# Layer 0's patch spectra in half-array matmuls: two patches in the halves of TensorE's rows, the inverse in the halves of its columns

## The chip, the cores and the metric

One core of a Trainium2 chip (trn2). The metric is the device time of one execution in microseconds (us), the median of several runs. A profile of one execution stands beside it. Lines are those of the kernel before; L512 is line 512. The engines: PE is TensorE's matmuls, PEld its weight loads, DVE is VectorE, ACT ScalarE, POOL GpSimd, SP SyncE.

## The reference, cut to what matters

`x` is 4 images of 48 channels and 256 x 256 pixels, fp32. Four layers follow, each added to its input after a group norm: layer 0 (below), layer 1 (a filter in 8 x 8 patches, a depthwise 3 x 3 convolution, a gated product), layer 2 (box means over learned offsets, from an integral image), layer 3 (a gated convolution and a filter in patches). Layer 0 is

```python
hidden = conv1x1(group_norm(x), w_hidden) + b_hidden          # 48 -> 288 channels
qkv = depthwise3x3(hidden, w_dw) + b_dw
q, k, v = split(qkv, 3, axis=1)                               # 96 channels each
q_patch, k_patch = (t.reshape(B, 96, 32, 32, 8, 8) for t in (q, k))
out = irfft2(rfft2(q_patch) * rfft2(k_patch), s=(8, 8))
out = out.reshape(B, 96, 256, 256)
normed = (out - mean(out, axis=1)) / sqrt(var(out, axis=1) + 1e-5) * gamma + beta
x = x + conv1x1(v * normed, w_out) + b_out
```

The reshape cuts each channel's memory into runs of 64 numbers, so a "patch" is 64 neighbouring pixels of one image row, read as 8 x 8. The product of two spectra is a complex one; the inverse of it is the circular convolution of the two patches.

## The kernel before, in words

The kernel is one program of fully unrolled Python loops under a tile framework, which adds the semaphores, gives tiles their buffers and orders each engine's instructions by a priority that follows the program order. Two streams of work are written into one order. Stream "a" runs layers 0 and 1 of image 0, then of images 1, 2, 3, and at the end layer 3 of all four; stream "b" runs the first statistics, layer 1's weights and layer 2 of each image as soon as layer 1 is done with it. `run` (the loop over `advance`) always takes up the stream whose clock is behind; each generator's `yield n` adds n to its clock. So the instructions of b that stand between two pieces of a are fixed by these numbers and not by the time on the chip, and each engine works its own list in order.

PSUM has 8 banks: a pool of 5 for stream a, 2 for stream b and one for layer 2's weights. `bank()` takes one of the stream's pool; a bank is free again when all that reads it is done.

Layer 0 (`layer0`) handles an image in 128 units of 512 pixels (4 blocks of 128). Its loop runs units n in a software pipeline: in step n it issues

- `convolve` of unit n: the 1x1 and 3x3 convolutions as one matmul over (tap, channel) rows, with pixels as the stationary operand and the 288 output channels moving. `convolve2` has 12 calls on 128 rows (L427) and 4 "tails" on 58 rows (L435), of which two in turn stand in rows 0 to 57 and in rows 64 to 121. Output: 4 banks of 128 pixels x 288 channels, copied by ACT to `qkv` (L508).
- `inverse` of unit n - 2 (L528, L529), then per channel statistics over 96 channels on DVE (`bn_stats`, L531) and a copy of the bank to `o` on ACT (L532); `scales` for a finished pair of units.
- a `yield`, at which stream b may put its instructions in between.
- `spectra` of unit n - 1 (L512 to L520), `turn` of unit n - 5 (4 transposes, L567), `project` of unit n - 6 for every second pair of units (L579), and `gate` of unit n - 4, and a second `yield`.

In `qkv` a partition is a pixel: partitions 0 to 63 are one patch, 64 to 127 the next. A patch of real numbers has 34 real and 30 imaginary parts that matter, 64 numbers. Before the change the two patches of a block share each matmul by a block-diagonal matrix of 128 x 128: `f1` gives in its 128 rows of output both patches' 68 real and 60 imaginary parts. `f2` gives for the products' other half the partners. `spectra` does three matmuls of 128 rows into 128 columns with 384 moving numbers (4 blocks x 96 channels): f1 on q, f1 on k and f2 on k. ACT copies q's spectrum to SBUF (`qs`, L516), DVE makes the two products t1 and t2 (L519, L520) and `inverse` adds a1 on t1 and a2 on t2 in one bank. An fp32 matmul is two instructions on PE in the profile (1024 where the program calls 512).

Of the kernel before, what the change touches and what calls it, by code (L numbers as in the profile page):

```python
# [8 lines left out]
F32 = mybir.dt.float32  # L9
# [49 lines left out]
def constants():  # L59
    own, pairs = _frequencies()  # L60
    every = own + pairs
    cos = {f: _waves(f)[0].ravel() for f in every}
    sin = {f: _waves(f)[1].ravel() for f in every}

    f1, f2, a1, a2 = (np.zeros((128, 128)) for _ in range(4))
    for k in range(2):
        px = slice(64 * k, 64 * k + 64)
        for i, f in enumerate(every):  # L70
            r, w = 34 * k + i, (1 if f in own else 2) / 64
            f1[px, r] = cos[f]
            a1[r, px] = w * cos[f]
            if f in pairs:
                f2[px, r] = -sin[f]
                a2[r, px] = -w * sin[f]
        for i, f in enumerate(pairs):
            r, w = 68 + 30 * k + i, 2 / 64
            f1[px, r] = -sin[f]
            f2[px, r] = cos[f]  # L80
            a1[r, px] = -w * cos[f]
            a2[r, px] = -w * sin[f]

    rf, pick = np.zeros((128, 128)), np.zeros((40, 128))
    at = [(f, True) for f in every] + [(f, False) for f in pairs]
    for j, (f, even) in enumerate(at):
        wave = (cos if even else sin)[f].reshape(8, 8) * (1 if f in own else np.sqrt(2)) / 8
        for k in range(2):  # L90
            block = np.zeros((8, 16))
            block[:, 8 * k : 8 * k + 8] = wave
            rf[:, 64 * k + j] = block.ravel()
            u, v = f
            if f in own or v in (1, 2, 3):
                pick[5 * u + v, 64 * k + j] = 1
            else:
                pick[5 * u + v, 64 * k + j] = pick[5 * (8 - u) + v, 64 * k + j] = 0.5

    sel = np.zeros((CP, 4, 112))
    tapsel = np.zeros((112, 4, 106))
    for g in range(4):
        for p in range(112 if g < 3 else 96):
            if g < 3:
                tap, ch = 3 * (p // 48) + g, p % 48
            else:
                tap, ch = 6 + p // 32, 16 + p % 32
            tapsel[p, g, 96 + tap] = 1  # L110
            sel[ch, g, p] = 1


    sel2 = np.zeros((CP, 4, 122))
    tapsel2 = np.zeros((128, 4, 74))
    sel2_full = np.zeros((CP, 3, 128))
    for g in range(3):
        for p in range(128):
            tap, ch = 3 * (p // 48) + g, p % 48
            sel2_full[ch, g, p] = 1  # L120
            for q in (0, 64):
                tapsel2[p, g, q + tap] = 1
    for p in range(48):
        sel2[32 + p % 16, 3, [10 + p, 74 + p]] = 1
        for q in (0, 64):
            tapsel2[10 + p, 3, q + 6 + p // 16] = 1
    sel2 = np.concatenate([sel2_full.reshape(CP, -1), sel2[:, 3]], 1)


    inside = np.ones((10, 256, PW))  # L130
    for t in range(9):
        if t // 3 == 0:
            inside[t, 0] = 0
        if t // 3 == 2:
            inside[t, -1] = 0
        if t % 3 == 0:
            inside[t, :, 0] = 0
        if t % 3 == 2:
            inside[t, :, 255] = 0

    group = np.zeros((CP, CP))
    for i in range(CP):
        for h in range(2):
            j = 48 * h + i % 48 // 3 * 3
            group[i, j : j + 3] = 1 / 6


    edge = np.zeros((10, 18), int)
    edge[1:9, 1:17] = np.arange(128).reshape(8, 16)
    edge[0, 1:17], edge[9, 1:17] = 128 + np.arange(16), 144 + np.arange(16)  # L150
    edge[1:9, 0], edge[1:9, 17] = 160 + np.arange(8), 168 + np.arange(8)
    edge[0, 0], edge[0, 17], edge[9, 0], edge[9, 17] = 176, 177, 178, 179
    shift = np.zeros((9, 128 + NH, 128))
    for r in range(8):
        for c in range(16):
            for t in range(9):
                shift[t, edge[r + t // 3, c + t % 3], 16 * r + c] = 1


    at128 = np.arange(128)[:, None]  # L160
    down = np.zeros((128, 2, 2, 129))
    along = np.zeros((128, 2, 256))
    for a in range(2):
        for h in range(2):
            down[:, h, a] = 128 * a + at128 <= 128 * h + np.arange(129)[None]
        along[:, a] = 128 * a + at128 <= np.arange(256)[None]


    px = at128 + 128 * np.arange(512)[None]
    centre = np.stack([(px % 256 + 0.5) / 256 * 2 - 1, (px // 256 + 0.5) / 256 * 2 - 1], 1)  # L170
    got = {
        "c_ident": np.eye(128),
        "c_dft": np.stack([f1, f2, a1, a2, rf, rf.T], 1),
        "c_pick": pick,
        "c_sel": sel,
        "c_tapsel": tapsel,
        "c_sel2": sel2,
        "c_tapsel2": tapsel2,
        "c_inside": inside.reshape(10, 256 * PW),
        "c_group": group,  # L180
        "c_shift": shift.reshape(9, -1),
        "c_down": down,
        "c_along": along,
        "c_centre": centre,
    }
    return {k: np.ascontiguousarray(v, dtype=np.float32) for k, v in got.items()}


class Net:
    def __init__(self, ctx, tc, a, out):  # L190
        self.tc, self.nc, self.a, self.out = tc, tc.nc, a, out
        self.nimage = a["x"].shape[0] // C

        self.banks = {
            f: ctx.enter_context(tc.tile_pool(name="ps" + f, bufs=n, space=PSUM)) for f, n in (("a", 5), ("b", 2))
        }
        self.stream = "a"
        self.const = ctx.enter_context(tc.tile_pool(name="const", bufs=1))
        self.dram = ctx.enter_context(tc.tile_pool(name="dram", bufs=1, space=DRAM))
        self.stat = ctx.enter_context(tc.tile_pool(name="stat", bufs=2))  # L200
        self.n = 0
        nc, a = self.nc, self.a
        self.ident = self.load("c_ident", [128, 128])
        dft = self.load("c_dft", [128, 6, 128])
        self.f1, self.f2, self.a1, self.a2, self.rf, self.ri = (dft[:, i, :] for i in range(6))
        self.sel = self.load("c_sel", [CP, 4, 112])
        self.tapsel = self.load("c_tapsel", [112, 4, 106])
        self.group = self.load("c_group", [CP, CP])
        self.eps = self.const.tile([128, 1], F32, name="eps")
        nc.vector.memset(self.eps[:], 1e-5)  # L210
        self.zero = self.const.tile([CP, PW + 4], F32, name="zero")
        nc.vector.memset(self.zero[:], 0.0)
# [253 lines left out]
    def layer0(self, x, mr, y):  # L466
        nc, a = self.nc, self.a
        st = self.stat.tile([CP, 129, 6], F32, name=self.nm("st"), tag="st" + self.stream, bufs=1)
        with ExitStack() as ctx:
            w = ctx.enter_context(self.pool("w0", 1))  # L470
# [37 lines left out]
                        nc.scalar.copy(t.qkv[:, 2 * q + b, :], banks[2 * b + q][:, 0:288])  # L508

            def spectra(t):  # L510
                q1, k1, k2 = self.bank(), self.bank(), self.bank()
                nc.tensor.matmul(v3(q1), self.f1, t.qkv[:, :, 0:96], start=True, stop=True)  # L512
                nc.tensor.matmul(v3(k1), self.f1, t.qkv[:, :, 96:192], start=True, stop=True)
                nc.tensor.matmul(v3(k2), self.f2, t.qkv[:, :, 96:192], start=True, stop=True)
                qs = sb.tile([128, 384], F32, name="qs", tag="qs")
                nc.scalar.copy(qs[:], q1[:, 0:384])  # L516
                t.t1 = sb.tile([128, 384], F32, name="t1", tag="t1")
                t.t2 = sb.tile([128, 384], F32, name="t2", tag="t2")
                nc.vector.tensor_mul(t.t1[:], qs[:], k1[:, 0:384])  # L519
                nc.vector.tensor_mul(t.t2[:], qs[:], k2[:, 0:384])  # L520

            def inverse(t):

                if t.j == 0:
                    t.strip.o = sb.tile([128, 8, 96], F32, name="o", tag="o")
                    t.strip.bs = sb.tile([128, 8, 6], F32, name="bs", tag="bs")
                po = self.bank()
                nc.tensor.matmul(po[:, 0:384], self.a1, t.t1[:], start=True, stop=False)  # L528
                nc.tensor.matmul(po[:, 0:384], self.a2, t.t2[:], start=False, stop=True)  # L529
                for b in range(4):  # L530
                    nc.vector.bn_stats(t.strip.bs[:, 4 * t.j + b, :], po[:, 96 * b : 96 * b + 96])  # L531
                nc.scalar.copy(  # L532
                    t.strip.o[:, 4 * t.j : 4 * t.j + 4, :].rearrange("p a b -> p (a b)"), po[:, 0:384]
                )
# [837 lines left out]
```

## Time and profile before

| what | before |
|---|---|
| median of 3 runs | 20871.12 us (20867.39 to 20881.85) |
| profiled execution | 20882.08 us, span from the first to the last instruction 20880.3 us |
| granted TensorE clock, mean | 0.922 |
| layer 0, first to last copy of qkv, images 0 to 3 | 130 to 1939, 3604 to 5592, 7798 to 9795, 12004 to 14000 us |
| layer 3 (first to last gelu, L1167) | 16207 to 20854 us |
| layer 2's gathers beside it (L1037), images 0 to 3 | 4050 to 7421, 8251 to 11630, 12456 to 15816, 16701 to 19831 us |

How to read the profile's views: a group of instructions is one line of the kernel on one engine with one kind of tile; "busy" is the time in which at least one of the group ran, "mean ns" the mean duration of one, and what follows the second bar is the time the engine stood idle just before them, with what ended it. Matmuls are pipelined, so durations of neighbours overlap and the distance from start to start says what one costs. In a view in order of time each row is a start, a length, the engine, the line, and how many instructions in turn were merged.

### The profile page before, as it was taken

To read this page: it belongs to the slowest core of one execution; us is meant where nothing else is said; L and a number is where in the kernel's file an instruction comes from. 1 tells how busy PE (TensorE), PEld (TensorE's weight loads), DVE (VectorE), ACT (ScalarE), POOL (GpSimd) and SP (SyncE) were. 2 spreads that over 40 slices of the span, in tenths; PEclk is the share of its full clock that TensorE was granted. 3 is DMA by queue.
4 is the path that set the end of the run, shared out by engine and by line. 5 is a ranking of instruction groups with operands and counts; after the bars stand their busy time and mean duration, and the time that the engine had idled before them with its cause. 6 is when DMAs were issued, how large, how long until landed. Compare 5 with 4: busy or idle time off the path is not lost.

```text
span 20880.3 us, 231985 instructions
## 1 busy us (share of the span) xinstructions
PE 18892.3 (90%) x79032; PEld 12001.4 (57%) x79032; DVE 10763.0 (52%) x21931; ACT 5909.3 (28%) x12275; POOL 8637.2 (41%) x8887
## 2 busy tenths in 40 slices
PE   7998798999878989998788899997888999999999
PEld 4565435666533346665433466654334787878888
DVE  4544322477765534677645447776554255555521
ACT  2333312344321123443311234433112211111111
POOL 1000000277754511777555216775552066666600
PEclk9899799999968999999689899996899999999999
DMA  4623886555588975555889755558897566666633
GB/s 114 135 55 82 233 217 194 137 132 134 132 235 230 241 207 139 130 134 127 233 230 240 219 133 130 133 127 229 236 239 225 137 150 151 158 152 160 151 76 74
DMA packets 2444896, 3440.27 MB, mean 165 GB/s; under 512 B 580102, under 2 KB 1997038, under 8 KB 2333179
## 3 DMA queue, kind: packets, MB, share of 16 engines
q1 hardware_dynamic: 1908216, 2084.50, 38.2%
q0 software_dynamic: 452560, 1110.45, 21.1%
q10 hardware_dynamic: 82944, 230.48, 4.4%
q8 instruction: 635, 10.40, 0.2%
q14 instruction: 541, 4.43, 0.1%
HBM read 2486.99 MB, written 802.77 MB: 158 GB/s over the span
## 4 chain that ended last, share of the span: by engine, by line
PE 65%; DMA 15%; DVE 7%; POOL 7%; issue 4%; SPq 1%; ACT 1%; DVEq 0%; ACTq 0%; POOLq 0%
PE ps L427 19%; POOL V L1037 7%; PE ps L947 6%; PE ps L728 5%; PE ps L435 4%; PE ps L741 4%; DMA ct<-cD 4%; PE ps L742 3%; PE ps L697 3%; PE ps L828 3%; DMA hD<-hs 2%; PE ps L1188 2%; DVE V L1050 2%; PE ps L815 1%; PE ps L966 1%
## 5 line engine op out<-in xcount | busy, mean ns | idle before, releaser
L1037 POOL DMA_INDIRECT V<-t,idx x8192 | 8227.0, 1004 | 4897.9 <-issue 2346.8
L427 PE MATMUL ps<-W,A 128*128 128x288 f32 (+1 forms) x24576 | 5547.3, 374 | 85.9 <-DMA A<-x 23.4
L427 PEld LDWEIGHTS ps<-W,A 128*128 128x128 f32 x24576 | 4281.6, 191 | 1226.6 <-issue 523.4
L227 POOL DMA_DIRECT2D X<-x x192 | 144.5, 757 | 4302.6 <-DMA x<-xt 3040.1
L1050 DVE TENSOR_TENSOR V<-V 128x1536 f32<-128x1536 f32 (+3 forms) x2048 | 1839.3, 900 | 19.2
L1048 DVE TENSOR_TENSOR V<-V,w 128x3072 f32<-128x3072 f32 x512 | 1713.3, 3346 | 35.9 <-DMA V<-t,idx 27.0
L728 PE MATMUL ps<-hg,ct 128*128 128x512 f32 x2304 | 1264.4, 676 | 417.5 <-DMA ct<-cD 339.5
L947 PE MATMUL ps<-A,W 112*96 112x512 f32 x3072 | 1544.9, 642 | 26.2 <-DVE xt L1069 21.5
L697 PE MATMUL ps<-win,xp 48*128 48x288 f32 x4096 | 1054.8, 594 | 547.9 <-DVE xp L684 232.4
L508 ACT COPY qkv<-ps 128x288 f32<-128x288 f32 x2048 | 769.9, 400 | 2641.1 <-PE ps L427 1258.4
L435 PE MATMUL ps<-W,B 58*128 58x288 f32 (+1 forms) x8192 | 1271.5, 391 | 26.1 <-DMA B<-x 13.8
L742 PE MATMUL ps<-yh,ht 65*128 65x512 f32 x2304 | 1163.1, 649 | 145.7 <-DMA yh<-ys 111.6
L531 DVE BATCH_NORM_STATS2 bs<-ps 128x6 f32<-128x96 f32 x2048 | 397.4, 251 | 1634.3 <-PE ps L529 1632.3
L741 PE MATMUL ps<-ys,tt 128*128 128x512 f32 x2304 | 1174.1, 632 | 27.6 <-DVE ys L732 25.7
L697 PEld LDWEIGHTS ps<-win,xp 48*128 48x128 f32 x4096 | 647.3, 259 | 924.3 <-ACT hs L704 291.9
L1168 DVE TENSOR_TENSOR gp<-gl,ps 128x192 f32<-128x192 f32 x1024 | 353.8, 351 | 1588.1 <-ACT gl L1167 1579.9
L728 PEld LDWEIGHTS ps<-hg,ct 128*128 128x128 f32 x2304 | 468.0, 211 | 1051.6 <-issue 949.1
L1167 ACT ACTIVATE gl<-ps 128x192 f32<-128x192 f32 x1024 | 332.7, 330 | 2529.4 <-PE ps L427 2245.4
L435 PEld LDWEIGHTS ps<-W,B 58*128 58x128 f32 x8192 | 762.4, 186 | 454.1 <-issue 346.4
L746 DVE TENSOR_TENSOR gt<-gl,ps 128x512 f32<-128x512 f32 x576 | 395.1, 687 | 1142.2 <-PE ps L742 1136.6
L947 PEld LDWEIGHTS ps<-A,W 112*96 112x96 f32 x3072 | 513.9, 176 | 731.4 <-issue 690.3
L742 PEld LDWEIGHTS ps<-yh,ht 65*128 65x128 f32 x2304 | 451.3, 199 | 794.3 <-issue 699.4
(186 smaller groups left out, 24654.4 us busy)
## 6 DMA issues: line engine op xcount, KB each, us to landing
hD<-hs SPq DMA_DIRECT2D x64, 4608.0 KB
hg<-hD SPq DMA_DIRECT2D x288, 1024.0 KB
gD<-gt SPq DMA_DIRECT2D x144, 1024.0 KB
gs<-gD SPq DMA_DIRECT2D x64, 2304.0 KB
V<-t,idx POOLq DMA_INDIRECT x8192
A<-x SPq DMA_DIRECT2D x512, 193.5 KB
xt<-x SPq DMA_DIRECT2D x256, 387.0 KB
A<-x ACTq DMA_DIRECT2D x512, 193.5 KB
```

The lines of the kernel that those rows point to most:

```text
L427: nc.tensor.matmul(to(q, b), A[:, r + q, 128 * b + g : 128 * b + g + 128], W[:, g, :], start=b == 0 and g == 0, stop=b == 1 and g == 2,)
L435: nc.tensor.matmul(to(q, b), B[p, r // 2, 128 * b : 128 * b + 128], W[p, 3, :], start=b == 1, stop=b == 0)
L508: nc.scalar.copy(t.qkv[:, 2 * q + b, :], banks[2 * b + q][:, 0:288])
L697: nc.tensor.matmul(ps[:, :288], xp[64 * h : 64 * h + 48, b, :], win[64 * h : 64 * h + 48], start=True, stop=True,)
L728: nc.tensor.matmul(ps[:].rearrange("p (s n) -> p s n", n=32), ct[:, c, :], hg[:, :, c, :], start=True, stop=True)
L741: nc.tensor.matmul(order(ps[:]), to[:, q, :], pick(yo, 128, q), start=True, stop=False)
L742: nc.tensor.matmul(order(ps[:]), ho[:, q, :], pick(yho, NZ, q), start=False, stop=True)
L828: nc.tensor.matmul(pp[:CP, :], pr[:, q, :], got[q][:], start=q == 0, stop=q == 2)
L947: m = nc.tensor.matmul(ps[:96, :].rearrange("p (r c) -> p r c", c=256), W[: kk[g], g, :], of[: kk[g]], start=g == 0, stop=g == 3,)
L1037: nc.gpsimd.indirect_dma_start(out=V[:, k, 4 * cr : 4 * cr + 4, :].rearrange("p e c -> p (e c)"), out_offset=None, in_=table, in_offset=ba ...
L1048: self.pinned(nc.vector.tensor_mul(Vm, Vm, wm.unsqueeze(2).to_broadcast([128, 64, 48])))
L1050: nc.vector.tensor_add(V[:, :, 0:n, :], V[:, :, 0:n, :], V[:, :, n : 2 * n, :])
```

## The change

Only layer 0's spectra, its inverse and the matrices for them change. There are no block-diagonal matrices any more, but matrices of 64 pixels for one patch. The first, `fq`, gives [f1 | f1]: the 64 numbers of the spectrum, twice; `fk` gives [f1 | f2]. The two halves of the partitions, that is the two patches of a block, are handled by separate matmuls on 64 rows each (rows 0 to 63 and 64 to 127), with an output of 128 partitions in a bank of their own. So q and k take two banks each. For each patch ACT copies q's bank to SBUF and DVE multiplies it with k's bank: one product of 128 x 384 holds both t1 and t2 of that patch. The inverse multiplies it with [a1; a2] (128 rows to 64 columns), patch 0 to PSUM partitions 0 to 63, patch 1 to partitions 64 to 127 of one bank, each in a single call instead of two that add up.

Per unit: spectra's calls 3 on 128 rows before, 4 on 64 rows after; inverse's calls 2 into 128 columns before, 2 into 64 columns after; banks in spectra 3 before, 4 after; copies of q on ACT 1 before, 2 after (each 128 x 384); products on DVE 2 before and after. Buffers for q's copy and the products: two each of 128 x 384 under one tag per patch.

```diff
-    f1, f2, a1, a2 = (np.zeros((128, 128)) for _ in range(4))
-    for k in range(2):
-        px = slice(64 * k, 64 * k + 64)
...
+    f1, f2, a1, a2 = np.zeros((64, 64)), np.zeros((64, 64)), np.zeros((64, 64)), np.zeros((64, 64))
...
+    first, second = np.tile(np.hstack([f1, f1]), (2, 1)), np.tile(np.hstack([f1, f2]), (2, 1))
+    back = np.vstack([a1, a2])
...
-        "c_dft": np.stack([f1, f2, a1, a2, rf, rf.T], 1),
+        "c_dft": np.hstack([first, second, rf, rf.T, back]),
...
-        dft = self.load("c_dft", [128, 6, 128])
-        self.f1, self.f2, self.a1, self.a2, self.rf, self.ri = (dft[:, i, :] for i in range(6))
+        dft = self.load("c_dft", [128, 576])
+        self.fq, self.fk, self.rf, self.ri = (dft[:, 128 * i : 128 * i + 128] for i in range(4))
+        self.back = dft[:, 512:576]
...
-                q1, k1, k2 = self.bank(), self.bank(), self.bank()
-                nc.tensor.matmul(v3(q1), self.f1, t.qkv[:, :, 0:96], start=True, stop=True)
-                nc.tensor.matmul(v3(k1), self.f1, t.qkv[:, :, 96:192], start=True, stop=True)
-                nc.tensor.matmul(v3(k2), self.f2, t.qkv[:, :, 96:192], start=True, stop=True)
-                qs = sb.tile([128, 384], F32, name="qs", tag="qs")
-                nc.scalar.copy(qs[:], q1[:, 0:384])
-                t.t1 = sb.tile([128, 384], F32, name="t1", tag="t1")
-                t.t2 = sb.tile([128, 384], F32, name="t2", tag="t2")
-                nc.vector.tensor_mul(t.t1[:], qs[:], k1[:, 0:384])
-                nc.vector.tensor_mul(t.t2[:], qs[:], k2[:, 0:384])
+                q, k = [self.bank() for _ in range(2)], [self.bank() for _ in range(2)]
+                half = lambda p: slice(64 * p, 64 * p + 64)
+                for to, f, c in ((q, self.fq, 0), (k, self.fk, 96)):
+                    for p in range(2):
+                        nc.tensor.matmul(
+                            v3(to[p]), f[half(p), :], t.qkv[half(p), :, c : c + 96], start=True, stop=True
+                        )
+                t.product = []
+                for p in range(2):
+                    qs = sb.tile([128, 384], F32, name="qs", tag=f"qs{p}")
+                    nc.scalar.copy(qs[:], q[p][:, 0:384])
+                    t.product.append(sb.tile([128, 384], F32, name="tp", tag=f"tp{p}"))
+                    nc.vector.tensor_mul(t.product[p][:], qs[:], k[p][:, 0:384])
...
-                nc.tensor.matmul(po[:, 0:384], self.a1, t.t1[:], start=True, stop=False)
-                nc.tensor.matmul(po[:, 0:384], self.a2, t.t2[:], start=False, stop=True)
+                for p in range(2):
+                    nc.tensor.matmul(
+                        po[64 * p : 64 * p + 64, 0:384], self.back, t.product[p][:], start=True, stop=True
+                    )
```

More of the change, by code (lines that the diff above doesn't have):

```diff
@@ L63, in constants @@
     sin = {f: _waves(f)[1].ravel() for f in every}
-    f1, f2, a1, a2 = (np.zeros((128, 128)) for _ in range(4))
-    for k in range(2):
-        px = slice(64 * k, 64 * k + 64)
[L70 to L82, printed above, removed]
+    f1, f2, a1, a2 = np.zeros((64, 64)), np.zeros((64, 64)), np.zeros((64, 64)), np.zeros((64, 64))
+    for i, f in enumerate(every):
+        w = (1 if f in own else 2) / 64
+        f1[:, i] = cos[f]
+        a1[i] = w * cos[f]
+        if f in pairs:
+            f2[:, i] = -sin[f]
+            a2[i] = -w * sin[f]
+    for i, f in enumerate(pairs):
+        f1[:, 34 + i] = -sin[f]
+        f2[:, 34 + i] = cos[f]
+        a1[34 + i] = -2 / 64 * cos[f]
+        a2[34 + i] = -2 / 64 * sin[f]
+    first, second = np.tile(np.hstack([f1, f1]), (2, 1)), np.tile(np.hstack([f1, f2]), (2, 1))
+    back = np.vstack([a1, a2])
     rf, pick = np.zeros((128, 128)), np.zeros((40, 128))
```

## The prediction, made before the changed kernel was run

> **What bounds the kernel now.** I read the page's busy row first, then the busy time by stage, then the groups of instructions, then the order of time inside one step of layer 0.
>
> ```profile
> PE 18892.3 (90%) x79032; PEld 12001.4 (57%) x79032; DVE 10763.0 (52%) x21931; ACT 5909.3 (28%) x12275; POOL 8637.2 (41%) x8887
> ```
>
> TensorE is the busiest engine, but 90% is a mean over stages. Layer 0 runs in four stretches (first to last copy of qkv, one per image); the second view has the engines' busy time in the first two of them (columns: length, then PE, PEld, DVE, ACT, POOL, granted clock, DMA share, GB/s).
>
> ```profile
> core 0: us, PE busy (x) PEld busy (x) DVE busy (x) ACT busy (x) POOL busy (x), PEclk, DMA share, GB/s
> 130.00:1950.00 1820.00, 1792.55 (x6527) 1093.79 (x6526) 798.91 (x2489) 657.97 (x1607) 72.81 (x138) 0.94 0.36 86
> 3604.00:5613.00 2009.00, 1980.74 (x8135) 1267.33 (x8134) 1280.67 (x2951) 812.46 (x1770) 1131.55 (x1129) 1.00 0.52 132
> ```
>
> PE is busy for 98.5% of both; DVE for 64% and POOL for 56% of the second, where layer 2 of another image runs beside. The third and fourth stretches read like the second. The four make 7865 us, and in them a microsecond of PE is a microsecond of the end, unless a wait takes its place.
>
> The groups of the changed lines, and two that resemble what comes (count | busy, mean ns of one | idle before):
>
> ```profile
> L427 PE MATMUL ps<-W,A 128*128 128x288 f32 (+1 forms) x24576 | 5547.3, 374 | 85.9 <-DMA A<-x 23.4 <-DVE xt L581 19.2 <-DVE z L1203 9.1
> L435 PE MATMUL ps<-W,B 58*128 58x288 f32 (+1 forms) x8192 | 1271.5, 391 | 26.1 <-DMA B<-x 13.8 <-DVE t L519 11.4 <-ACT qkv L508 0.5
> L512 PE MATMUL ps<-qkv,c_dft_sb 128*128 128x384 f32 x1024 | 424.7, 497 | 0.0
> L529 PE MATMUL ps<-t,c_dft_sb 128*128 128x384 f32 x1024 | 416.0, 488 | 0.0
> L516 ACT COPY qs<-ps 128x384 f32<-128x384 f32 x512 | 244.8, 478 | 544.6 <-PE ps L512 451.3 <-issue 32.4 <-DMA A<-x 18.8
> ```
>
> 512 units (128 per image) give 1024 matmuls a line: each fp32 matmul is two passes on PE. L435 already does what the change wants for the spectra: its two calls stand in rows 0 to 57 and 64 to 121. Its matmuls last 391 ns each but cover only 1271.5/8192 = 155 ns apiece; L427's cover 5547.3/24576 = 226. They overlap in pairs.
>
> One step in order of time, PE alone (start us, us, what):
>
> ```profile
> 1003.28 0.81 PE L528 MATMUL ps<-t,c_dft_sb 128*128 128x384 f32 x2
> 1003.92 0.81 PE L529 MATMUL ps<-t,c_dft_sb 128*128 128x384 f32 x2
> 1004.57 0.81 PE L512 MATMUL ps<-qkv,c_dft_sb 128*128 128x384 f32 x2
> 1005.21 0.81 PE L513 MATMUL ps<-qkv,c_dft_sb 128*128 128x384 f32 x2
> 1005.86 0.81 PE L514 MATMUL ps<-qkv,c_dft_sb 128*128 128x384 f32 x2
> 1006.50 0.60 PE L567 MATMUL ps<-c_ident_sb,un 128*96 128x128 f32 x4
> ...
> 1008.66 3.08 PE L427 MATMUL ps<-W,A 128*128 128x288 f32 x12
> 1011.66 1.24 PE L435 MATMUL ps<-W,B 58*128 58x288 f32 x8
> 1012.83 3.18 PE L427 MATMUL ps<-W,A 128*128 128x288 f32 x12
> 1015.85 0.81 PE L528 MATMUL ps<-t,c_dft_sb 128*128 128x384 f32 x2
> ```
>
> From L528 to L567 ten passes take 6.50 - 3.28 = 3.22 us: 0.322 us a pass of 384 columns, start to start, with no gap and all weight loads hidden. A pass of 288 columns should then be 0.322 x 288/384 = 0.2415 us.
>
> **Removed and added passes.** Before: 6 passes in spectra, 4 in inverse, 10 x 0.322 = 3.22 us a unit. After: spectra has 4 calls on 64 rows (8 passes), inverse 2 calls into 64 columns (4 passes). If two halves run at once, spectra is 4 slots, inverse 2: 6 x 0.322 = 1.93 us. Four slots go: 4 x 0.322 x 512 = 659 us.
>
> For the row halves the trace decides: eight passes of L435 take 1012.83 - 1011.66 = 1.17 us; in turn they would take 1.93. For the column halves no row exists: no matmul here writes PSUM from partition 64 with 64 columns or fewer. Bounds: full overlap 0.64 us, as L435; none 1.29 us, as now; over 512 units the two ends differ by 2 x 0.322 x 512 = 330 us. I take full overlap, since L435 is the nearest row, with the same two calls in turn and the same fp32. The doubt is that each partition's data must now be read for two tiles at once, which L435 doesn't do.
>
> **Switches between shapes.** From 1008.66 to 1015.85 there are 24 full passes and 4 slots of pairs: 28 x 0.2415 = 6.76 us, but 7.19 passed. The 0.43 us are the two changes of shape, full to halves and back, 0.21 us each. The Trainium skill (TensorEngine Tiling (Array Packing), Key Properties) says that a change of tiling mode, unlike a change of tile, drains the engine. It speaks against this change and names no price; the row gives it. Left out, the sum would be 659 us; by the row it is halved, as follows. Today spectra and inverse have the convolution's shape and need no switch. After, the order is full, columns, rows, full: 3 switches a unit. In 345 of 512 units L512 follows L529 directly; in 167 a matmul of the other stream stands between, and there it is a fourth. 3 x 512 + 167 = 1703 switches x 0.21 = 358 us. Columns to rows isn't in the trace; I give it the same price (bounds 0.1 and 0.3, so about 50 us to either side).
>
> 659 - 358 = 301 us less PE.
>
> A second rule against it: the skill's TensorE: Matmul & The Clock Gate (Part 3, The mechanism) says weight loads overlap running matmuls only when the row group differs; both column tiles use all rows. By its rule of columns/1.2 ns, four loads of 64 columns are 0.21 us a unit if exposed, an estimate of 109 us. The trace disagrees: L528 to L514 load 128 columns ten times in 3.22 us without a gap, on the same rows. I charge nothing, and keep 109 us for the range.
>
> **ACT and DVE.** One copy of q more per unit: 478 ns x 512 = 245 us on ACT, which is busy 36 to 40% in these stretches: hidden in its idle time; uncovered it would cost all 245. The DVE products stay two of 128x384 (549 ns each, L519 and L520). The constants are loaded once, 576 columns for 768: nothing.
>
> **The banks: a possible new wait.** Stream a has 5 PSUM banks. In spectra the inverse's bank and three others were held, and the transposes (L567) had a free fifth. Now spectra holds four, so L567 must wait until the inverse's bank or the first q bank is free. Behind L567 on PE wait project and the next convolution. The timeline of such a unit:
>
> ```profile
> 4825.18 0.81 PE L529 MATMUL ps<-t,c_dft_sb 128*128 128x384 f32 x2
> ...
> 4826.02 0.76 DVE L531 BATCH_NORM_STATS2 bs<-ps 128x6 f32<-128x96 f32 x4 [7.70 <-PE ps L529]
> ...
> 4826.66 0.48 ACT L516 COPY qs<-ps 128x384 f32<-128x384 f32 x1 [1.54 <-PE ps L512]
> ...
> 4827.04 0.49 ACT L532 COPY o<-ps 128x384 f32<-128x384 f32 x1
> ```
>
> The last inverse pass starts at 4825.50; its bank is free 2.03 us later, at 4827.53. In the new order L567 is due 0.32 + 0.21 + 1.29 + 0.21 = 2.03 us after it: just in time. The first q bank is ready earlier: q's pair ends about 1.33 us after that pass, plus a 0.48 us copy. But DVE and ACT may be held by others. Over all 512 units the release comes on average 2.46 us after; had every L567 to wait for that bank, the mean wait would be 0.52 us, against some 65 us in all (0.13 each) that PE waits for that copy now: +0.39 x 512 = 200 us. At the other end nothing, as the q bank serves. I take 0.1 us a unit, 50 us, nearer to nothing as q's copy usually comes in time. Products held late by DVE (L435 already waits 40 us for them) come about as late as now.
>
> **Sum.** 301 - 50 = 251 us. The profiled execution is 20882.08 us, its span 20880.3; the median is 20871.1, 11 below. 20882 - 251 - 11 = 20620 us, -1.2%.
>
> **Rivals.**
> 1. Column halves run in turn. PE then loses 301 - 330 = 29 us, and with 50 us of waits the kernel is 79 us slower: 20950. Place: the two calls of inverse; it decides once they need over 0.64 + 251/512 = 1.13 us of the possible 1.29. For it: no row of the trace, two streams from each partition. Against: L435's calls of the same form overlap fully. If only the middle passes overlap (3 slots), half is lost: 251 - 165 = 86, 20785.
> 2. The bank wait takes the place: 301 - 200 = 101 us faster, 20770. For it: five banks, all held; 10% of the releases come over 3.85 us after. Against: the q bank.
> 3. DVE or POOL sets the pace where layer 2 runs beside, and only the first image gains: 251 x 1820/7865 = 58 us, 20813. Against: 64% and 56% busy.
> 4. The halves don't do what they say and rows run in turn: 4 more slots, 659 us lost. L435 excludes it.
>
> **Chances.** Main case 0.56, its own range 20530 (no bank wait, switches into 64 columns some 0.05 us cheaper) to 20700 (switches at 0.25 us or so); rival 1 in full 0.22, by half 0.07; rival 2 0.12; rival 3 0.03. The range 20530 to 20945 leaves out about half of rival 1 and a little below: under 2 in 10. About 0.2% can be told from no change, 42 us either way. Faster: the main case and what of the others stays under 20829, 0.70. Within: remains of rivals 1 to 3, 0.08. Slower: rival 1, 0.22.
>
> **What would show it.** The inverse's new line should cover about 160 ns a pass (0.64 us for its four), its two calls starting within some ns; 320 ns means rival 1. The four spectra calls should take 1.29 us from first to last plus the two edges. From the last convolution pass to L567, 2.6 us for 3.22 where no other stream's work lies between. PE's waits before L567 for L532 or the q copy: under 100 us, over 200 is rival 2. The layer-0 stretches should each be some 60 us shorter, layers 1 and 3 unchanged. I am wrong most simply if a pair of columns, or a change from columns to rows, costs more than L435's.

## The result, and the profile after

The changed kernel takes 20835.58 us (median of 20 runs) against 20877.06 us for the kernel before in 20 runs: a ratio of 0.9982, interval 0.9975 to 0.9989. (One run of each took over twice as long, 53574 and 42591 us, and is left out of the ratio.) That is a gain of 41 us where 251 were forecast. It lies inside the range; it is small, but the interval leaves no change out. The profiled execution took 20836.07 us (span 20834.3, mean granted clock 0.917). Lines are now those of the kernel after: the inverse is L534, its statistics L538 and the copy to `o` L539; spectra is L517, the copies of q L523, the products L525, the transposes L574, the projection L586, the convolution L428 and its tails L436.

The page's busy row: TensorE is busy for 300 us less than before.

```profile
PE 18592.2 (89%) x80056; PEld 11483.9 (55%) x80056; DVE 10767.5 (52%) x21931; ACT 6091.5 (29%) x12787; POOL 8608.8 (41%) x8887
```

The same two windows as before the change (length, PE, PEld, DVE, ACT, POOL, granted clock, DMA share, GB/s). In the first, PE has room; in the second it is busy for 1888 of 2009 us where it was for 1981, and its clock has gone from 1.00 to 0.97. The second window ends 73 us behind the changed kernel's own stretch, which is 3531 to 5540 us; that one has 1910 us of PE and a clock of 0.98 (its line stands with the first experiment).

```profile
130.00:1950.00 1820.00, 1742.90 (x6936) 981.51 (x6934) 837.42 (x2565) 723.85 (x1781) 73.18 (x138) 0.92 0.37 90
3604.00:5613.00 2009.00, 1887.85 (x8092) 1111.56 (x8092) 1308.12 (x2983) 844.09 (x1847) 1159.98 (x1153) 0.97 0.52 131
```

The changed groups of matmuls: a third more passes than before in spectra (4096 for 3072), as many as before in the inverse.

```profile
L517 PE MATMUL ps<-qkv,c_dft_sb 64*128 64x384 f32 x4096 | 848.0, 517 | 5.0 <-ACT qkv L509 5.0
L534 PE MATMUL ps<-tp,c_dft_sb 128*64 128x384 f32 x2048 | 447.3, 514 | 15.3 <-DVE tp L525 15.3
```

One step of image 0 in order of time, PE alone. The four passes of the inverse take 0.79 us to the next start, the eight of spectra 1.50. From the inverse to the transposes it is 2.29 us.

```profile
1028.38 0.87 PE L534 MATMUL ps<-tp,c_dft_sb 128*64 128x384 f32 x4
1029.17 1.56 PE L517 MATMUL ps<-qkv,c_dft_sb 64*128 64x384 f32 x8
1030.67 0.64 PE L574 MATMUL ps<-c_ident_sb,un 128*96 128x128 f32 x4
```

So the matmuls do what was hoped; the time goes elsewhere. Worked out from the start times and clock rows of the two traces, for the layer-0 stretch of each image (first to last copy of qkv): its length; the time in it at half clock; and the sum of PE's standstills, which counts each start-to-start distance over 0.75 us, less 0.35 for a pass. A pass of 512 columns takes 0.86 us at half clock and so counts as well: 76 and 82 us of image 0's two sums are of this kind, and 15 us or less of each of the others.

| image | length before | after | half clock before | after | standstills before | after |
|---|---|---|---|---|---|---|
| 0 | 1808.8 | 1746.0 | 228.7 | 273.1 | 109.7 | 140.1 |
| 1 | 1988.1 | 2008.8 | 6.8 | 88.7 | 26.9 | 113.0 |
| 2 | 1997.1 | 2006.1 | 17.1 | 81.9 | 33.9 | 112.6 |
| 3 | 1996.7 | 2003.3 | 17.1 | 75.1 | 33.8 | 108.4 |

Image 0, which has no layer 2 beside it, gains 63 us. The other three are longer by 21, 9 and 7. One of their standstills, in order of time (in brackets how long the engine stood, and for whom):

```profile
4310.98 3.35 DVE L1055 TENSOR_TENSOR V<-V,w 128x3072 f32<-128x3072 f32 x1
...
4311.69 1.56 PE L517 MATMUL ps<-qkv,c_dft_sb 64*128 64x384 f32 x8
...
4314.24 0.75 DVE L538 BATCH_NORM_STATS2 bs<-ps 128x6 f32<-128x96 f32 x4
...
4315.10 0.48 ACT L539 COPY o<-ps 128x384 f32<-128x384 f32 x1 [3.69 <-DVE bs L538]
4315.48 0.87 ACT L523 COPY qs<-ps 128x384 f32<-128x384 f32 x2
...
4315.63 0.64 PE L574 MATMUL ps<-c_ident_sb,un 128*96 128x128 f32 x4 [2.38 <-ACT o L539]
```

DVE is in layer 2's product for 3.35 us (L1055) and reaches the inverse's statistics only then. ACT stands 3.69 us in front of the copy to `o`, because that copy reads the same bank and is made to follow the statistics. Both copies of q stand behind it in ACT's list, although their banks have been full for more than a microsecond. So no bank is free until `o` has been copied, and PE stands 2.38 us in front of the transposes. At 4316.7 us the granted clock falls to half, for 3.4 us.

What ACT and PE wait for in the stretch of image 1 (total us, times, longest), first ACT, then PE, both of the kernel after:

```profile
ACT o L539 <- DVE bs L538: 99.5, 56, 7.0
```

```profile
PE ps L428 <- ACT qs L523: 18.3, 12, 5.4
PE ps L586 <- ACT qs L523: 15.6, 11, 2.2
PE ps L574 <- ACT o L539: 14.7, 10, 3.2
PE ps L428 <- DVE tp L525: 14.2, 5, 5.9
```

And ACT's wait in the same stretch of the kernel before:

```profile
ACT o L532 <- DVE bs L531: 94.8, 52, 4.1
```

ACT's wait for DVE is old: 94.8 us in 52 times. But the fifth bank was free then, and PE stood only 4.3 us for ACT's copies of q and `o`. In the kernel after ACT's wait is on PE's path, and through the banks it reaches the projection and the next convolution as well. The last of PE's rows is a second kind: a bank of k, which is free only when DVE has made the product. Over the whole kernel PE's waits for ACT's copies of q and `o` went from 15.7 to 164.6 us, those for DVE's products from 26.8 to 72.6.

### The profile page after: what moved, and what is told of

Same layout as the page of the kernel before. It is cut to its first block, busy times and chain, and to the rows that moved or that the text cites. A ratio compares the mean times of both kernels' runs of the same rounds, so it can differ in the third digit from the quotient of the medians.

```text
span 20834.3 us, 235001 instructions
## 1 busy us (share of the span) xinstructions
PE 18592.2 (89%) x80056; PEld 11483.9 (55%) x80056; DVE 10767.5 (52%) x21931; ACT 6091.5 (29%) x12787; POOL 8608.8 (41%) x8887
## 4 chain that ended last, share of the span: by engine, by line
PE 62%; DMA 16%; DVE 9%; POOL 7%; issue 4%; SPq 1%; ACT 1%; ACTq 0%; DVEq 0%; POOLq 0%
PE ps L428 19%; POOL V L1044 7%; PE ps L954 5%; PE ps L735 4%; PE ps L436 4%; PE ps L748 4%; DMA ct<-cD 3%; PE ps L749 3%; PE ps L704 3%; PE ps L835 3%; PE ps L1195 2%; DVE V L1057 2%; DVE V L1055 2%; DMA hD<-hs 2%; PE ps L517 2%
## 5 line engine op out<-in xcount | busy, mean ns | idle before, releaser
L428 PE MATMUL ps<-W,A 128*128 128x288 f32 (+1 forms) x24576 | 5612.7, 378 | 184.3 <-ACT qs L523 52.8
L428 PEld LDWEIGHTS ps<-W,A 128*128 128x128 f32 x24576 | 4329.6, 193 | 1351.8 <-issue 554.8
L1055 DVE TENSOR_TENSOR V<-V,w 128x3072 f32<-128x3072 f32 x512 | 1713.9, 3347 | 39.8 <-DMA V<-t,idx 31.7
L436 PE MATMUL ps<-W,B 58*128 58x288 f32 (+1 forms) x8192 | 1239.7, 392 | 28.5 <-DVE tp L525 14.3
L538 DVE BATCH_NORM_STATS2 bs<-ps 128x6 f32<-128x96 f32 x2048 | 398.3, 253 | 1615.1 <-PE ps L534 1614.7
L436 PEld LDWEIGHTS ps<-W,B 58*128 58x128 f32 x8192 | 751.8, 187 | 440.1 <-issue 329.6
L711 ACT COPY hs<-ps 128x288 f32<-128x288 f32 x1024 | 619.3, 657 | 1006.1 <-PE ps L704 824.3
```

Source lines behind the costliest of these rows:

```text
L428: nc.tensor.matmul(to(q, b), A[:, r + q, 128 * b + g : 128 * b + g + 128], W[:, g, :], start=b == 0 and g == 0, stop=b == 1 and g == 2,)
L436: nc.tensor.matmul(to(q, b), B[p, r // 2, 128 * b : 128 * b + 128], W[p, 3, :], start=b == 1, stop=b == 0)
L1055: self.pinned(nc.vector.tensor_mul(Vm, Vm, wm.unsqueeze(2).to_broadcast([128, 64, 48])))
```

## The experiments

The theory ahead of the first runs: the matmuls save what they should, and the lost time is PE waiting for a bank that ACT frees late. Rivals: DVE, with layer 2 beside, sets the pace whatever the banks do; the saving itself is small where another stream interleaves; or half-array matmuls bring the granted clock down by themselves.

**The copy to `o` first, and the statistics from SBUF.** ACT then waits for the matmul alone. DVE's work stays the same in number and size.

```diff
-                for b in range(4):
-                    nc.vector.bn_stats(t.strip.bs[:, 4 * t.j + b, :], po[:, 96 * b : 96 * b + 96])
                 nc.scalar.copy(
                     t.strip.o[:, 4 * t.j : 4 * t.j + 4, :].rearrange("p a b -> p (a b)"), po[:, 0:384]
                 )
+                for b in range(4):
+                    nc.vector.bn_stats(t.strip.bs[:, 4 * t.j + b, :], t.strip.o[:, 4 * t.j + b, :])
```

> The changed kernel, but ACT's copy of the inverse's bank to o comes first and bn_stats reads o in SBUF, so that the bank waits for ACT alone and no longer for DVE. Theory A (the gain is lost where the transposes and the next convolution wait for a bank that is released behind DVE's long layer-2 instructions, with ACT's copy of o standing ahead of the q copies): most of the lost gain comes back, 20540 to 20680 us, and waits of PE over 0.4 us in layer 0 of image 1 fall from 142 us to under 80. Theory B (DVE's or ACT's own pace sets the layer-0 stretches where layer 2 runs beside): 20800 us or more. Theory C (half-array matmuls bring the granted clock down by themselves): at most 60 us better, and the clock stays at about 0.97 in these stretches.

The same edit in the kernel before:

> The kernel before with the same reordering of copy and statistics, as the control. Theory A: PE waits little for that copy here (some 65 us in all), so 20810 to 20880 us. Theories B and C: no change, 20850 to 20890 us.

Measured: in the changed kernel 20626.45 us, 0.9878 (0.9863 to 0.9894); in the kernel before 20852.25 us, 0.9985 (0.9975 to 0.9994). With the copy first in both, the change is worth 226 us; without, 41. The stretches of images 1 to 3 are 65, 73 and 71 us shorter than in the kernel after; image 0's is as long as there (1749 us). PE's waits in image 1 and the stretch's busy times in the kernel with the copy first:

```profile
PE ps L586 <- ACT qs L523: 6.4, 6, 2.0
PE ps L428 <- ACT qs L523: 4.6, 6, 2.0
```

```profile
3537.00:5481.00 1944.00, 1891.36 (x8337) 1133.25 (x8337) 1260.12 (x2923) 858.24 (x1878) 1140.98 (x1112) 0.98 0.54 135
```

For comparison the same stretch of the kernel after:

```profile
3531.00:5540.00 2009.00, 1909.53 (x8336) 1139.95 (x8336) 1268.44 (x2920) 849.45 (x1878) 1109.81 (x1113) 0.98 0.51 131
```

DVE does the same 1260 to 1268 us of work in 1944 us as in 2009, so its amount of work is not what makes the stretch 2009 us long. The transposes' wait for `o` (14.7 us) is gone from the list. Standstills fall from 113.0 to 67.1 us and half clock from 88.7 to 61.4.

**Layer 2 left out.** Both kernels compute layers 0, 1 and 3 only; their outputs lack layer 2.

```diff
-        Net(ctx, tc, aps, out).run()
+        Net(ctx, tc, aps, out).run((0, 1, 3))
```

> The kernel before without layer 2 (left out altogether; layers 0, 1 and 3 alone), the base for the next run: 18500 to 20000 us by no theory in particular; layer 0's stretches of images 1 to 3 shorter by layer 2's share of PE.

> The changed kernel without layer 2 (left out altogether). Against the run before it: theories A and B give the full gain in all four images, 250 to 410 us faster (410 = 512 units x 0.81 us less of PE, less what is lost in waits). Theory C gives under 120 us, with a granted clock in the layer-0 stretches clearly below that of the run before it.

Measured: 16997.82 us with the old spectra, well under the 18500 to 20000 expected, and 16641.53 with the new: the change saves 356 us. The stretch of image 1, old spectra and new:

```profile
3590.00:5069.00 1479.00, 1479.00 (x6065) 984.01 (x6065) 561.82 (x1738) 570.20 (x1442) 0.00 (x0) 1.00 0.21 49
```

```profile
3541.00:4920.00 1379.00, 1379.00 (x6320) 846.45 (x6320) 565.09 (x1738) 606.64 (x1568) 0.00 (x0) 1.00 0.22 53
```

PE is busy throughout, at full clock, in both; so the half-array matmuls do not lower the clock by themselves. The stretch is 100.5 us shorter, 0.785 us for each of 128 units. This is the change's own worth without a wait. Five banks are enough when DVE and ACT come in time; layer 2 beside them makes them late. Image 0, which has no layer 2 beside it in either case, gains only 54 us here: what it loses has another cause.

**Only ACT's list changed.** The statistics stay on PSUM; the copy to `o` is moved behind the two copies of q in ACT's list (`pinned` keeps it at its place).

```diff
-                nc.scalar.copy(
-                    t.strip.o[:, 4 * t.j : 4 * t.j + 4, :].rearrange("p a b -> p (a b)"), po[:, 0:384]
-                )
+                t.po = po
...
+            def keep(t):
+                self.pinned(nc.scalar.copy(
+                    t.strip.o[:, 4 * t.j : 4 * t.j + 4, :].rearrange("p a b -> p (a b)"), t.po[:, 0:384]
+                ))
...
                     spectra(unit(n - 1))
+                if unit(n - 2):
+                    keep(unit(n - 2))
```

> The changed kernel with ACT's copy of o pinned behind both q copies. Where the kernel before takes about 20880 us: theory A1 (the order of ACT's list costs) 20640 to 20740 us; theory A2 (the inverse's bank must come free early) 20800 us or more.

Measured: 20787.71 us, 0.9949 (0.9935 to 0.9962), some 69 us better than the change as it stands (0.9982 to 0.9949 of 20890), and a third of what the copy first brings. That meets neither expectation: it lies between them. In 66 of 127 steps of image 1 in the kernel after, ACT's list has the copy to `o` ahead of both of q's; here never. But the standstills hardly fell (110.9 us in image 1, from 113.0), and now PE waits for q. Of the 57 us by which the four stretches together are shorter, standstills (4 us less) and half clock (41 us less, worth at most 20) give 24; the rest isn't placed. One of these waits, in order of time:

```profile
4125.44 1.56 PE L517 MATMUL ps<-qkv,c_dft_sb 64*128 64x384 f32 x8
...
4125.55 3.40 ACTq L305 DMA_DIRECT2D B<-x  x3
...
4129.39 0.86 ACT L523 COPY qs<-ps 128x384 f32<-128x384 f32 x2 [3.22 <-DMA B<-x]
```

ACT also issues the convolution's loads (L302 to L306), and three of them kept its list for 3.40 us; q's copies stand behind those. The issues themselves took 0.3 to 0.4 us each; before the second, ACT stood 2.2 us until an earlier load (A) had landed. Of the 23 standstills before the transposes in image 1, 12 have such loads on ACT around spectra's last matmul and the copy; what held the others was not followed up. So whichever copy comes first, PE waits for the one bank, and something in ACT's list may hold it. With the copy to `o` first and independent of DVE, two banks come free by two ways, and before the transposes of images 1 to 3 a single standstill of 0.4 us is left.

**A sixth bank.** Layer 2's weights go to SBUF, and their PSUM bank to stream a; in both kernels.

```diff
-            f: ctx.enter_context(tc.tile_pool(name="ps" + f, bufs=n, space=PSUM)) for f, n in (("a", 5), ("b", 2))
+            f: ctx.enter_context(tc.tile_pool(name="ps" + f, bufs=n, space=PSUM)) for f, n in (("a", 6), ("b", 2))
...
-            weights = self.banks[self.stream].tile([128, 2, 256], F32, name=self.nm("w4"), tag="w4", bufs=1)
+            weights = w.tile([128, 2, 256], F32, name="w4")
```

> The changed kernel with 6 banks for stream a and w4 in SBUF. Where the kernel before takes about 20880 us: theory A (banks) 200 us or more below the next run; theory B (DVE's or ACT's pace) within 60 us of it.

> The kernel before with 6 banks and w4 in SBUF, the control. 20840 to 20900 us if w4's place has no effect of its own; it gave 1.3 to 1.4% less where all kernels were held back.

Measured: the changed kernel 20887.36 us, 0.9996 (0.9987 to 1.0005); the kernel before 21008.91 us, 1.0050 (1.0034 to 1.0065). With six banks in both, the change saves 122 us, against 41 with five: more than the 60 of the one theory, less than the 200 of the other. Before the transposes of images 1 to 3 standstills fall from 49.1 to 3.4 us, but all standstills of image 1 together stay (115 us, from 113). The bank is worth some 80 us to the changed kernel, but taking it costs more: the kernel before, which did not need it and was expected at 20840 to 20900 us, lost about 119 us. The groups of the gathers and of DVE's product with the weights (count, busy, mean ns, idle before) in the kernel before with six banks, then as it was:

```profile
L1037 POOL DMA_INDIRECT V<-t,idx x8192 | 9447.7, 1153 | 3875.3 <-issue 2384.8 <-DVE res L1051 1098.9 <-DVE idx L1010 195.7
L1048 DVE TENSOR_TENSOR V<-V,w 128x3072 f32<-128x3072 f32 x512 | 1716.5, 3352 | 366.2 <-DMA V<-t,idx 347.4 <-issue 15.1 <-DMA x<-xt 0.4
L1037 POOL DMA_INDIRECT V<-t,idx x8192 | 8227.0, 1004 | 4897.9 <-issue 2346.8 <-DVE res L1051 1979.6 <-DVE idx L1010 192.4
L1048 DVE TENSOR_TENSOR V<-V,w 128x3072 f32<-128x3072 f32 x512 | 1713.3, 3346 | 35.9 <-DMA V<-t,idx 27.0 <-DVE w L1022 2.7 <-issue 2.6
```

An issue of a gather takes 15% longer on POOL, and DVE stands 347 us for the gathers' data where it stood 27. The two kernels differ in the sixth bank and in the weights' place: DVE's product of layer 2 now reads both inputs from SBUF. Its own duration is unchanged (3346 ns before, 3352). The Trainium skill (GPSIMD Engine Reference, Specifications) says that POOL shares its SBUF interfaces with VectorE and meets contention from instructions with two SBUF inputs; it gives no size for it. The longer issues fit that, but that they come from the weights' place and not from the bank, and that they make the whole 119 us, was not isolated.

**The same on two other chips.** There the kernel before takes 25729.97 and 25380.93 us. On the first of them:

> The changed kernel with ACT's copy of o pinned behind both q copies of the same step; bn_stats still reads PSUM and comes before it. Nothing else changes, so the inverse's bank is released later, the q banks earlier. Theory A1 (the order of ACT's list is what costs: a copy of o that waits for DVE holds back the q copies, whose banks the transposes and the next matmuls could take): 20640 to 20740 us. Theory A2 (the inverse's bank itself must come free early): 20800 us or more, as without it one bank fewer goes round.

> The changed kernel with 6 PSUM banks for stream a; the sixth comes from layer 2's weights w4, which stand in SBUF instead. Theory A (banks): the transposes have a free bank again, as before the change; 20600 to 20740 us, provided that the run after this one stays within 40 us of the kernel before. Theory B: 20800 us or more.

> The kernel before with the same sixth bank and w4 in SBUF, the control: 20840 to 20900 us if the weights' place does not matter to DVE and a sixth bank relieves nothing that binds; if DVE's layer-2 products change with w4 in SBUF it shows in their mean duration (3346 ns before).

Measured: 0.9963 (0.9944 to 0.9981), 0.9853 (0.9834 to 0.9872) and 0.9858 (0.9839 to 0.9878). A further kernel there has row halves alone: the copy first, and an inverse with full matrices padded with zeros, into 128 columns.

```diff
-    back = np.vstack([a1, a2])
+    back = np.zeros((128, 256))
+    for p in range(2):
+        back[:, 192 * p : 192 * p + 64] = np.vstack([a1, a2])
...
-        self.back = dft[:, 512:576]
+        self.back = [dft[:, 512 + 128 * p : 640 + 128 * p] for p in range(2)]
...
-                        po[64 * p : 64 * p + 64, 0:384], self.back, t.product[p][:], start=True, stop=True
+                        po[:, 0:384], self.back[p], t.product[p][:], start=p == 0, stop=p == 1
```

> The reordered version of the changed kernel (copy first, 20626 us) with the row halves alone: the inverse again has two full-array calls that add up in one bank, with matrices padded by zeros. Per unit 8 slots of 0.322 us and two switches instead of 6 slots and three: about 0.64 - 0.16 = 0.48 us more of PE, 246 us over 512 units; theory: 20790 to 20870 us, that is, most of the gain is the columns'. If a switch cost 0.21 us or more as I had forecast, it would be nearer 20770.

Measured: 1.0006 (0.9994 to 1.0017). On the second of these chips the first three again, and six banks with the copy first:

> The kernel of a_qfirst once more, since that chip held all engines of all kernels back in the stretches with layer 2 (25730 us for the kernel before) and hid the difference. Where the kernel before takes about 20880 us: theory A1 (the order of ACT's list costs) 20640 to 20740 us; theory A2 (the inverse's bank must come free early) 20800 us or more.

> The kernel of a_six once more (6 banks, w4 in SBUF), for the same reason. Theory A (banks) 20560 to 20740 us; theory B 20800 us or more. It is to be held against the next run, since w4's place may change DVE's part.

> The kernel of b_six once more, control for a_six_2. Theory A: 20840 to 20900 us; the slow chip gave 1.4% less than the kernel before for both, so w4 in SBUF may have an effect of its own, to be seen here (then 20580).

> The changed kernel with both remedies, the copy of o first and a sixth bank with w4 in SBUF. If both take away the same wait, at most 60 us below the better of them, 20520 to 20630 us; floor by PE: kernel before less 410 us, 20470 us. If w4 in SBUF has a gain of its own, down to 20300 us.

Measured: 0.9970 (0.9959 to 0.9981), 0.9887 (0.987 to 0.9904), 0.9864 (0.9848 to 0.988) and 0.9872 (0.9855 to 0.9889). There the six banks help the kernel before as much as the changed one, and say nothing of the change. On these chips images 1 to 3 take 2612 to 2715 us in layer 0 instead of 2000, and the stages of layers 1 and 3 beside gathers are longer too; as long as layer 2's gathers run, the engines but for POOL stand much of the time for nothing that the profile names. No time expected for a chip of 20880 us can be held against these. Image 0 is as on the other chips, so only that part can be read: from the last convolution pass to the second transpose a unit undisturbed by other work and at full clock takes 3.58 us before (median), 3.27 with row halves alone and 2.77 with both. The rows give 0.31 us, the columns 0.50.

## Why the prediction was right or wrong

**Passes: right.** Both kinds of halves overlap fully. Two calls of the column halves start 6 to 7 ns apart (1028.379 and 1028.385 us, 1028.753 and 1028.759), so rival 1, in full or by half, is out.

**Switches: right in kind, too dear.** From the starts of neighbouring passes, full to columns costs 0.144 us, columns to rows 0.203, rows to the transposes 0.14: 0.49 us for the three that were put at 0.63. The price of 0.21 was right for the pair it was read from: the convolution to its tails and back costs 0.20 each way in both kernels. A unit is 0.81 us shorter where 0.66 was forecast, and 0.785 with layer 2 left out. In the 167 steps with another stream's matmul between inverse and spectra the fourth switch adds about 0.19 us, so the matmuls save some 0.81 x 512 - 0.19 x 167 = 383 us (an estimate from these starts), where the prediction had 301. Where another stream interleaves the saving is thus smaller, but only by 32 us in all. The switches alone cost 283 us, of the 358 forecast. That TensorE's busy time fell by 300 us, nearly the 301 of the prediction, is chance: half clock makes other passes longer.

**Weight loads: right.** The inverse's 0.79 us to spectra's first pass are two slots of 0.322 and 0.15 us that belong to the switches on its two sides; nothing is left for exposed loads, so the 109 us held for them fall away.

**ACT's copy: right as busy time only.** ACT is busy for 42% of image 1's stretch. But "hidden in its idle time" left out where in ACT's list the copies stand.

**Banks: the step that failed.** "I take 0.1 us a unit, 50 us, nearer to nothing as q's copy usually comes in time" was wrong. In 66 of 127 steps beside layer 2 q's copies stand behind the copy to `o`, which waits for DVE's statistics, which wait for layer 2's product. Two supposed ways to a free bank were one. In place of the 50 us the runs show 217: so much comes back when the copy to `o` no longer waits for DVE (0.9982 to 0.9878), 210 of it in the stretches of images 1 to 3. The prediction also had no term for the clock, which takes up to 124 us (below). And "products held late by DVE come about as late as now" did not hold: PE's waits for them went from 26.8 to 72.6 us.

The whole account: some 383 us saved by the matmuls less 41 measured is 342. In the table time at half clock grew by 44 + 82 + 65 + 58 = 249 us, which costs at most half, 124; standstills grew by 30 + 86 + 79 + 75 = 270, of which 35 are long passes at half clock that the clock's share has already. 383 - 124 - 235 leaves 24, and the four stretches together are 26.5 us shorter. Not all of this is the banks behind layer 2. By the same estimate image 0 lost some 37 us of its saving, and the copy first gives none of them back: there PE waits 3.1 us for copies of `o`, but 37.8 for the convolution's loads where it waited 20.7, and time at half clock grew. Images 1 to 3 lost some 320, of which the copy first gives back 210. Outside the stretches the changed kernel is some 15 us faster.

Three readings of the trace before were off, with little effect on the sum. PE's wait for that copy, put at 65 us, is 24.8 in the view of the copy's line (6.9 of PE, 17.9 of its weight loads), and the same edit makes the kernel before 28 us faster. The wait of L435 for the products, put at 40 us, is 28.2 (11.4 and 16.8). And the 7865 us of the four stretches are the lengths of the windows; from first to last copy of qkv they are 7791.

**Rival 2** named the mechanism, and its 200 us come near the 217. In part that is luck: it counted a mean delay of one release per unit and no clock, and of the 210 us in the stretches the clock has up to 53. **Rival 3** came nearest in time (20813) with the wrong cause: its mark, that only the first image gains, is what the table shows, but the copy first moves 217 us with DVE's work unchanged. For these 217 us it is DVE's lateness at single places, passed on by ACT, and not its amount of work.

**The marks.** Stretches some 60 us shorter: true of image 0 alone. "160 ns a pass" was badly put: 447.3/2048 is 218, because the busy time of a lone group includes the tail of its last pass (0.87 us in the row, 0.79 to the next start); start to start decides. The wait before the transposes, expected under 100 us, has 84.8 us on PE in the group of L574, and would have passed as harmless: the transposes took the next bank and handed the wait to the convolution and the projection. A mark has to count all that take a bank.

**Left open.** With the copy first the change is worth 226 us beside layer 2 and 356 without. Of the 110 us still lost in images 1 to 3 the waits name a part: over the whole kernel PE waits 45 us for DVE's products where it waited 27 before the change, and 35 for the copies of q and `o` where it waited 16; and half clock in these stretches is 140 us, from 41. No run takes these apart, and none has a remedy for DVE's late products or for image 0's loads. The kernel with the copy first is the best of all, 20626 us, 1.2% under the kernel before.

## What to carry to other kernels

When an edit takes the last spare buffer, follow each way by which the next one comes free through the list of the engine that frees it, instruction by instruction, to what that engine waits for; two ways through one in-order list are one way. A wait of 95 us that costs nothing today is what a tight pool will charge tomorrow. Let a bank have one reader that waits for nothing but the matmul, and make the second reader work from its copy.

## What the runs showed of the hardware that was not expected

- Short standstills can halve the clock. In image 1 the kernel after has 16 stretches at half clock, of 3.4 to 13.7 us, where the kernel before has 2; in 12 of the 16 PE had stood 1.8 to 3.3 us in one piece within the 4 us before. Not every such standstill does it: in images 1 to 3, of 49 that began at full clock 33 were followed by half clock within 4 us. The Trainium skill (TensorE: Matmul & The Clock Gate, Part 1: The HAM clock gate) asks for an idle window of about 3.4 us; here less than that in one piece was enough.
- Two column halves in fp32 run side by side, each with its own moving data: the two calls start 6 to 7 ns apart, and four passes take 0.79 us, that is, two slots of 0.322 and the switches.
- The price of a change of shape depends on the two shapes: 0.144 us from full to column halves, 0.203 from columns to rows, 0.14 from rows to the transposes, but 0.20 from rows to the convolution and from the convolution to rows.
- With layer 2's weights in SBUF in place of PSUM (and one more bank for stream a) another engine became slower: POOL's issue of a gather went from 1004 to 1153 ns; on the two other chips it was 1021 to 1030 with that edit and 976 to 978 without.
- On two of the chips every kernel that ran there had the gathers, and the kernel before took 22 to 23% longer; the time is lost in the stages beside gathers, and image 0's layer 0, without them, is as short as elsewhere (1745 us for 1739, both with ACT's list changed). The cause stays open.
